# A transformer block on one core: the attention's row sums move from GpSimd to ScalarE

## The chip, the core and the metric

The kernel runs on one core of a Trainium2 chip. The metric is device time of one execution in microseconds (us). Five engines work side by side, each through its own instructions in order: TensorE (PE in the profile, PEld for its weight loads), VectorE (DVE), ScalarE (ACT), GpSimd (POOL) and SyncE (SP), which here issues every DMA. They wait for each other through semaphores. PSUM, where TensorE leaves its products, has eight banks of 128 x 512 f32.

## The reference

Input x is (8, 1024, 512) f32. Each token is layer-normed; the normed xn goes through causal attention with 16 heads of 32 and, in parallel, through a gated network whose inputs and weights are rounded to a 4-bit grid in blocks of 16. The result is the sum of three:

```python
xn = _layernorm(x, axis=-1)
x = x + _L0_attn_ref(xn, W_attn, b_attn, W_proj, b_proj) + _L0_ffn_ref(xn, w_gate, w_up, w_down)

# attention, per head
att = softmax(where(causal, q @ k.T * HD**-0.5, -inf));  y = att @ v
# fp4_quant_dequant, in blocks of 16 along the last dim
scale = max(max(abs(xb)) / 6, 1e-12)
q = GRID[searchsorted(MID, abs(xb / scale))] * sign(xb) * scale
# network
h = silu(fp4_linear(x, w_gate)) * fp4_linear(x, w_up);  return fp4_linear(h, w_down)
```

The softmax needs, for each row of scores, its maximum and the sum of its exponentials. The change is about that sum.

## The kernel before, in words

**Pieces.** The 8 batches x 1024 tokens are 64 tiles of 128 tokens; the 8 batches x 16 heads are 64 units of two heads (`HU = 2`). So a batch has eight tiles and eight units. Work on a tile: `prepare` (layer norm, transposes, `project` to q, k and v, which go to DRAM), `quantised` (the tokens rounded to the grid and transposed, `xqT`), `network` (three chunks of the hidden width 1408: `product` with the gate and up weights, `gated`, `hidden`, then `turn` and `down`) and `finish` (projection of the attention's y, sum with the network, output). Work on a unit: `maxima` and `weigh`.

**Maxima.** For 128 queries by up to 512 keys, `maxima` lets TensorE compute a block of scores in fp32r into a PSUM bank (L538, 24 blocks per unit), VectorE add the causal mask to the diagonal part (L546) and reduce to the negated row maximum (L548). The maxima of a unit are split into two fp32r parts, transposed (L564), stored to DRAM, and loaded as rows `shT`.

**Weights.** `weigh` computes the scores again, transposed: a matmul of `pick` and `shT` puts the negated maxima into the bank (L657), the matmul of `ks` and `qs` adds the scores (L660), ScalarE takes the exponential into `pr` in SBUF (L668), GpSimd clears what lies above the diagonal (L674), and TensorE multiplies by the values into y (L639). The inner `summed` lets GpSimd add the `pr` tiles into `sums` (L628, L633). At the end of each half Q of a unit, matmuls with `ones` sum over the partitions (L706); the sums go to DRAM, come back in `invert`, are inverted by VectorE and stored as `inverses`, which `finish` loads as `inv_y`.

**Quantising.** `Quantised` is a chain of VectorE operations on one 128 x 512 piece (L300 to L324). For the first `EARLY` = 28 of the 34 weight pieces, its two multiplications by a broadcast scale (L320, L324) run on GpSimd instead.

**What sets the order.** All instructions stand in an order written out by a planner in the program itself. It keeps a clock, dates at which each engine comes free (`act`, `dve`, `pool` add a planned cost), and the date at which each of six rotating PSUM banks comes back (`Banks`). Each piece of work is a generator that yields (TensorE's cost, the date from which it can go on, how many banks it needs); `merge` lets that stream go on that is least far in its own progress among those that can start. `Later` puts an action at a planned date. The chip has none of these dates: it runs each engine's instructions in the order that came out, and waits. Main stage: for unit n, `maxima` starts at progress n - 1.3, `weigh` at n, the network of tile n at n + 2, `finish` at n + 10, and the tiles two batches ahead are prepared in pairs. Before it lies a head in which the first 16 tiles are prepared and 28 weight pieces quantised.

In PSUM the six rotating banks serve all products but two, y and acc, which have a bank each.

Of the kernel before, what the change touches and what calls it, by code (L numbers as in the profile page):

```python
# [27 lines left out]
def kernel(  # L28
# [51 lines left out]
    QUEUE = 2.0  # L80
    SURE = 0.4
# [35 lines left out]
    ones = const.tile([P, HD], F32, name="ones")  # L117
    nc.gpsimd.memset(ones, 1.0)
# [66 lines left out]
    class Banks:  # L185


        def __init__(self):
            self.tiles = [ps_g.tile([P, W], F32, name=f"bank{k}") for k in range(6)]
            self.at = [0.0] * 6  # L190

# [3 lines left out]
        def take(self):  # L195
            k = self.at.index(min(self.at))
            assert self.at[k] < float("inf")
            self.at[k] = float("inf")
            return k, self.tiles[k]

        def back(self, k, time):
            self.at[k] = time

# [47 lines left out]
    class Quantised:  # L251
# [11 lines left out]
        def __init__(self, src, w, xs, after=0.0, helper=False):  # L263
# [6 lines left out]
            for wide, us, engine, action in self.operations(src, w, xs, helper):  # L270
                us = us + wide * w / CW
                self.left.append(Later(start, lambda us=us, engine=engine, action=action: self.one(us, engine, action)))
                start += SPREAD * us
# [8 lines left out]

        def done(self):
# [6 lines left out]
        def operations(self, src, w, xs, helper):  # L290
# [6 lines left out]
            spreader, name, cost = (nc.gpsimd, "pool", 1.35) if helper else (nc.vector, "dve", 0.7)  # L297
# [6 lines left out]
            def powers():  # L304
# [14 lines left out]
                (0.25, 0.72, "dve", scales),  # L319
                (cost, 0.0, name, lambda: spreader.tensor_tensor(blocks(xs), blocks(src), spread(inv), ALU.mult)),  # L320
                (1.14, 0.0, "dve", powers),
                (0.74, 0.0, "dve", lambda: nc.vector.tensor_tensor(xs, xs, step, ALU.add)),
                (0.78, 0.0, "dve", lambda: nc.vector.tensor_tensor(xs, xs, step, ALU.subtract)),
                (cost, 0.0, name, lambda: spreader.tensor_tensor(blocks(xs), blocks(xs), spread(scale), ALU.mult)),  # L324
# [12 lines left out]
    def weights_quantised():  # L337
# [15 lines left out]
        for k, piece in enumerate(pieces):  # L353
            raw = loaded.pop(0)
            done.append((piece, Quantised(raw, piece[4], raw, helper=k < EARLY)))
            while len(done) > (1 if k + 1 < len(pieces) else 0):
                (_, dst, r, c, w), wq = done.pop(0)
                yield 0.0, wq.ready(), 1
# [13 lines left out]
    def normed(tl):  # L372
# [9 lines left out]
        yield 0.0, pool(0.6, dve(1.4)), 0  # L382
        nc.vector.tensor_scalar(xt, xt, mv[:, 0:1], rstd, ALU.subtract, ALU.mult)
        tl.ready = dve(0.72)
# [25 lines left out]
    def quantised(tl):  # L410
# [6 lines left out]
        yield 0.0, xq.ready(), 1  # L417
# [5 lines left out]
    def project(batch, g, after):  # L423
        xnT = batch.xnT
        yield 0.0, after, 1
        for s in range(2):
            for f in range(0, NC, 2):
# [28 lines left out]
                def split(full=full, high=high, low=low):  # L456
                    nc.vector.tensor_copy(high, full)
                    nc.vector.tensor_tensor(low, full, high.bitcast(F32), ALU.subtract)
                    dve(1.3)
# [62 lines left out]
    def maxima(un):  # L522
# [3 lines left out]
        neg = p2.tile([P, 3, NK], F32, name="neg")  # L526
        for t in range(NT):
# [3 lines left out]
            for r in range(HU):  # L531
                k = i * HU + r
                for h in range(Q + 1):
                    n = W if h < Q else (i + 1) * P
                    bank, sc = banks.take()
# [12 lines left out]
                    nc.vector.tensor_reduce(neg[:, Q + h, k : k + 1], sc[:, :n], AX.X, ALU.max, negate=True)  # L548
                    end = dve(0.16 + 0.00103 * n, end)
                    banks.back(bank, end)  # L550
                    yield cost, free["dve"] - QUEUE, 1
        nc.vector.tensor_tensor(neg[:, 1, :], neg[:, 1, :], neg[:, 2, :], ALU.min)

        high = p2.tile([P, 2, NK], F32R, name="neg_high")
        stat = p2.tile([P, 2, 2, HU, QG], F32, name="stat")
        by_head = lambda a: a.rearrange("p (i r) -> p r i", r=HU)
        nc.vector.tensor_copy(high, neg[:, :2, :])
        for q in range(2):
            nc.vector.tensor_copy(stat[:, 0, q], by_head(high.bitcast(F32)[:, q, :]))
            nc.vector.tensor_tensor(stat[:, 1, q], by_head(neg[:, q, :]), stat[:, 0, q], ALU.subtract)  # L560
        rows = 2 * 2 * NK
        yield 0.0, dve(2.6), 1, 0.3
# [7 lines left out]
        def store():  # L570
            un.shift = dram.tile([2, 2, HU, W], F32, name="shift_kept")
            nc.sync.dma_start(out=un.shift.rearrange("e q r (i p) -> (e q r i) p", p=P), in_=statT)
            Later(2.5, load)
# [10 lines left out]
        yield 0.15, 0.0, 0, 0.3  # L584

    def weigh(un):
# [16 lines left out]

        def invert():
            flat = HU * S // P
            z = p2.tile([P, flat], F32, name="z")
            nc.sync.dma_start(out=z, in_=un.batch.sums[un.u].rearrange("q g (p e) -> (q g p) e", e=flat))
            inverses = un.batch.inverses[un.u].rearrange("q r (p e) -> (q r p) e", e=flat)
            Later(14.0, lambda: nc.vector.reciprocal(z, z))

            def store():
                nc.sync.dma_start(out=inverses, in_=z)
                un.batch.units_done += 1

            Later(16.0, store)

        for Q in range(2):
# [3 lines left out]
            sums = [p1.tile([P, W], F32, name=f"sum{r}") for r in range(HU)]  # L621

            def summed(group):

                for r in range(HU):
                    prs = [(pr, q0) for _, s, pr, q0 in group if s == r]
                    if group[0][0] == 0:
                        nc.gpsimd.tensor_tensor(sums[r], prs[0][0], prs[1][0], ALU.add)  # L628
                        pool(1.35)
                    else:  # L630
                        for pr, q0 in prs:
                            pool(0.2 + (W - q0) * 0.0022)
                            nc.gpsimd.tensor_tensor(sums[r][:, q0:], sums[r][:, q0:], pr[:, q0:], ALU.add)  # L633

# [16 lines left out]
            for j in range(last + 1):  # L651
# [45 lines left out]
                if j % 2 == 1:  # L697
                    summed(waiting)
            yield 0.0, max(ready, emptied, free["pool"] + HOP), 1
# [23 lines left out]
            def store(Q=Q, yu=yu, zs=zs):  # L723
# [8 lines left out]
                if Q == 1:  # L732
                    Later(8.0, invert)
# [385 lines left out]
```

## Time and profile before

| | us |
|---|---|
| median of 3 runs | 4801.91 (4801.69 to 4806.67) |
| the profiled execution | 4794.69 |
| its span | 4792.7 |
| TensorE busy | 4317.5 (90%) |
| VectorE busy | 3332.4 (70%) |
| GpSimd busy | 1942.2 (41%) |
| ScalarE busy | 1473.8 (31%) |
| granted TensorE clock, mean | 0.958 |

Busy time of an engine counts its instructions from start to end; matmuls overlap and their ends are modelled, so a TensorE that is shown busy is not at its peak. A row of the costliest groups reads: line, engine, operation, what is written and read, shape and count, then busy time and mean ns of one, then the idle time of the engine just before these instructions and what ended it. A row of the waits reads: who waited, for what, then us in total, times, and the longest. "PE bank L331 <- DVE xs L324" is TensorE idle before a transpose (L331) until VectorE's last operation (L324) on the tile `xs` had ended.

### The profile page before, as it was taken

Reading aid. Unit: us, or ns where it says so; the run is one execution under the profiler, and the core shown is the slowest. Engines: PE = TensorE matmul, PEld = TensorE weight load, DVE = VectorE, ACT = ScalarE, POOL = GpSimd, SP = SyncE. Lnnn points to the kernel's source line nnn. Section 1 sums busy time; section 2 is a strip of 40 time slices with the busy share of each in tenths; the row PEclk is TensorE's granted clock in tenths of the full one; section 3 lists DMA queues with packets and bytes.
Section 4 is the critical chain, followed back from the end, with each engine's and each line's share of the span. In section 5 each row is a group of like instructions: output and inputs, shape, how many; then the busy total and the mean of one; then the engine's idle time right before and its main releaser. Section 6 shows DMA issues by size and latency. Waiting matters only on the chain.

```text
span 4792.7 us, 59517 instructions
## 1 busy us (share of the span) xinstructions
PE 4317.5 (90%) x18708; PEld 2664.7 (56%) x18708; DVE 3332.4 (70%) x6883; ACT 1473.8 (31%) x2910; POOL 1942.2 (41%) x2632
## 2 busy tenths in 40 slices
PE   6566999999999999999999999999999899999994
PEld 5454555555565555556655555655555555555553
DVE  5556767777777777777777677777777777777752
ACT  1112333333333333333333333333333333333320
POOL 2213444444444444444444444443444444444430
PEclk8788999999999999999999999999999999999997
DMA  5655434435444544554454454545544333333213
GB/s 185 204 166 143 109 108 119 107 112 143 135 131 140 141 135 128 148 137 132 136 150 135 125 150 131 141 131 144 139 125 105 97 85 85 85 85 85 76 58 92
DMA packets 601659, 596.99 MB, mean 125 GB/s; under 512 B 133504, under 2 KB 457600, under 8 KB 601344
## 3 DMA queue, kind: packets, MB, share of 16 engines
q1 hardware_dynamic: 601344, 593.18, 44.9%
q8 instruction: 150, 2.46, 0.2%
q14 instruction: 165, 1.35, 0.1%
HBM read 423.11 MB, written 169.87 MB: 124 GB/s over the span
## 4 chain that ended last, share of the span: by engine, by line
PE 52%; DVE 25%; DMA 15%; SPq 3%; issue 3%; ACT 1%; POOL 0%; DVEq 0%; ACTq 0%; POOLq 0%
PE bank L785 16%; PE acc L763 6%; PE bank L878 4%; PE bank L538 4%; PE bank L657 4%; PE bank L433 4%; PE y L639 4%; PE bank L660 4%; DMA ks<-qk_kept 3%; DMA qk_kept<-full 3%; DMA inv_y<-inv_kept 3%; DMA qs<-qk_kept 3%; PE bank L331 2%; DVE step L308 2%; PE bank L477 2%
## 5 line engine op out<-in xcount | busy, mean ns | idle before, releaser
L633 POOL TENSOR_TENSOR sum<-sum,pr 128x512 f32<-128x512 f32 (+3 forms) x1024 | 1000.1, 987 | 428.8 <-ACT pr L668 392.9
L548 DVE TENSOR_REDUCE neg<-bank 128x1 f32<-128x512 f32 (+3 forms) x1536 | 840.9, 556 | 348.3 <-PE bank L538 312.3
L668 ACT ACTIVATE pr<-bank 128x512 f32<-128x512 f32 (+3 forms) x1536 | 674.9, 491 | 1022.6 <-PE bank L660 848.6
L674 POOL TENSOR_SCALAR_AFFINE_SELECT pr<-pr 128x128 f32<-128x128 f32 x1024 | 388.7, 393 | 1225.9 <-ACT pr L668 1217.8
L538 PE MATMUL bank<-ks,qs 128*128 128x512 f32 (+3 forms) x1536 | 703.9, 505 | 53.1 <-DMA ks<-qk_kept 17.7
L785 PE MATMUL bank<-wuT,xqT 128*128 128x512 f32 (+1 forms) x1536 | 682.3, 571 | 0.0
L763 PE MATMUL acc<-wdT,hqT 128*128 128x512 f32 x1408 | 677.3, 602 | 1.4 <-ACT hqT L332 1.4
L785 PE MATMUL bank<-wgT,xqT 128*128 128x512 f32 (+1 forms) x1536 | 660.5, 563 | 0.0
L657 PE MATMUL bank<-shT,pick 128*128 128x512 f32 (+3 forms) x1536 | 605.7, 402 | 31.0 <-ACT full L444 25.2
L546 DVE TENSOR_TENSOR bank<-bank,mask 128x128 f32<-128x128 f32 x1024 | 299.3, 292 | 447.5 <-PE bank L538 446.5
L628 POOL TENSOR_TENSOR sum<-pr 128x512 f32<-128x512 f32 x256 | 362.4, 1440 | 608.2 <-ACT pr L668 608.2
L660 PE MATMUL bank<-qs,ks 128*128 128x512 f32 (+3 forms) x1536 | 520.8, 348 | 0.0
L433 PE MATMUL bank<-xnT,wa 128*128 128x256 f32 x2048 | 480.2, 390 | 5.1 <-DMA wa<-in_L_attn_W_attn_dram 3.5
L538 PEld LDWEIGHTS bank<-ks,qs 128*128 128x128 f32 x1536 | 284.4, 191 | 328.3 <-issue 195.3
L433 PEld LDWEIGHTS bank<-xnT,wa 128*128 128x128 f32 x2048 | 397.4, 197 | 73.3 <-DMA wa<-in_L_attn_W_attn_dram 5.5
L657 PEld LDWEIGHTS bank<-shT,pick 128*128 128x128 f32 x1536 | 294.1, 191 | 221.1 <-issue 106.2
L785 PEld LDWEIGHTS bank<-wgT,xqT 128*128 128x128 f32 x1536 | 279.9, 191 | 233.7 <-issue 180.6
L785 PEld LDWEIGHTS bank<-wuT,xqT 128*128 128x128 f32 x1536 | 283.5, 195 | 205.6 <-issue 161.2
L763 PEld LDWEIGHTS acc<-wdT,hqT 128*128 128x128 f32 x1408 | 257.9, 191 | 225.0 <-issue 208.8
L639 PE MATMUL y<-pr,vs 128*32 128x512 f32 (+3 forms) x3072 | 361.7, 518 | 0.0
L660 PEld LDWEIGHTS bank<-qs,ks 128*128 128x128 f32 x1536 | 294.7, 192 | 60.8 <-issue 31.8
L444 ACT ACTIVATE full<-bank,bqk 128x256 f32<-128x256 f32 x256 | 107.5, 471 | 608.6 <-DMA qk_kept<-full 299.4
(88 smaller groups left out, 4899.7 us busy)
## 6 DMA issues: line engine op xcount, KB each, us to landing
wa<-in_L_attn_W_attn_dram SPq DMA_DIRECT2D x192, 512.0 KB
qs<-qk_kept SPq DMA_DIRECT2D x512, 128.0 KB
ks<-qk_kept SPq DMA_DIRECT2D x512, 128.0 KB
wp<-in_L_attn_W_proj_dram SPq DMA_DIRECT2D x81, 512.0 KB
qk_kept<-high SPq DMA_DIRECT2D x128, 256.0 KB
qk_kept<-full SPq DMA_DIRECT2D x128, 256.0 KB
y_kept<-yu SPq DMA_DIRECT2D x256, 128.0 KB
yT<-y_kept SPq DMA_DIRECT2D x128, 256.0 KB
```

The lines of the kernel that those rows point to most:

```text
L433: nc.tensor.matmul(pq[:, j, :], lhsT=wa[:, c, j * P : (j + 1) * P], rhs=xnT[:, c, :], start=(c == 0), stop=(c == NC - 1),)
L538: nc.tensor.matmul(sc[:, :n], lhsT=un.qs[Q][:, r, i * P : (i + 1) * P], rhs=un.ks[h][:, r, :n], start=True, stop=True,)
L548: nc.vector.tensor_reduce(neg[:, Q + h, k : k + 1], sc[:, :n], AX.X, ALU.max, negate=True)
L628: nc.gpsimd.tensor_tensor(sums[r], prs[0][0], prs[1][0], ALU.add)
L633: nc.gpsimd.tensor_tensor(sums[r][:, q0:], sums[r][:, q0:], pr[:, q0:], ALU.add)
L639: nc.tensor.matmul(y[row : row + HD, q0:], lhsT=un.vs[h][:, jj, r * HD : (r + 1) * HD], rhs=pr[:, q0:], start=(j < 2), stop=(j >= last - 1 ...
L657: nc.tensor.matmul(w[:, q0:], lhsT=pick[:, Q * HU + r, :], rhs=un.shT[:, q0:], start=True, stop=False)
L660: nc.tensor.matmul(w[:, q0:], lhsT=un.ks[h][:, r, jj * P : (jj + 1) * P], rhs=un.qs[Q][:, r, q0:], start=False, stop=True,)
L668: nc.scalar.activation(pr[:, q0:], w[:, q0:], AF.Exp)
L674: nc.gpsimd.affine_select(out=pr[:, q0 : q0 + P], in_=pr[:, q0 : q0 + P], compare_op=ALU.is_ge, fill=0.0, base=0, pattern=[[1, P]], channe ...
L763: nc.tensor.matmul(tl.acc, lhsT=job.hqT[:, j, :], rhs=wdT[:, i, :], start=(i == 0), stop=(i == NI - 1))
L785: nc.tensor.matmul(job.g, lhsT=job.tl.xqT[:, c, :], rhs=wT[:, c, job.i0 : job.i0 + job.w], start=(c == 0), stop=(c == NC - 1),)
```

## The change

1. In `maxima`, after each block's maximum, ScalarE takes the exponential of the block in place in its PSUM bank, with the block's own negated maximum as bias, and gives the row sums through `accum_out`. The bank comes back after that. At a unit's end the two partial sums of a row are brought to the common maximum (`least`, `gap`, one small exponential), added, inverted, and transposed and stored together with the maxima (48 rows instead of 32).
2. `summed` on GpSimd, the ones matmuls, the copies `zs`, and the way of the sums through DRAM go. `yu` gets two buffers.
3. All weight pieces are quantised by VectorE alone.
4. In the planner: banks that are held are tracked; a stream that waits for a quantised tile asks again until the planned end has passed (`wait`); several planned costs of VectorE are lower; `units_done` counts when y is stored.

```diff
+    LATE = 0.6
...
-    ones = const.tile([P, HD], F32, name="ones")
-    nc.gpsimd.memset(ones, 1.0)
...
         def take(self):
-            k = self.at.index(min(self.at))
-            assert self.at[k] < float("inf")
+            while len(self.held) == len(self.tiles):
+                passed(0.2)
+            k = min((k for k in range(len(self.tiles)) if k not in self.held), key=self.at.__getitem__)
             self.at[k] = float("inf")
+            self.held.add(k)
             return k, self.tiles[k]
+        def expect(self, k, time):
+            self.at[k] = time
...
+        def wait(self):
+            while self.ready() > clock[0] + 0.05:
+                yield 0.0, self.ready(), 1
...
-            spreader, name, cost = (nc.gpsimd, "pool", 1.35) if helper else (nc.vector, "dve", 0.7)
...
-            done.append((piece, Quantised(raw, piece[4], raw, helper=k < EARLY)))
+            done.append((piece, Quantised(raw, piece[4], raw)))
...
-                yield 0.0, wq.ready(), 1
+                yield from wq.wait()
...
         xq = Quantised(xs, D, xs)
-        yield 0.0, xq.ready(), 1
+        yield from xq.wait()
...
+        sums = p2.tile([P, 3, NK], F32, name="row_sums")
+        older = []
+        def summed(bank, sc, n, kind, k):
+            nc.scalar.activation(
+                sc[:, :n],
+                sc[:, :n],
+                AF.Exp,
+                bias=neg[:, kind, k : k + 1],
+                accum_out=sums[:, kind, k : k + 1],
+            )
+            banks.back(bank, act(n, 0.0, "exp") + 0.27)
+            free["act"] += 0.27
...
-                    banks.back(bank, end)
+                    block = (bank, sc, n, kind, k)
+                    older.append(Later(end - clock[0] + LATE, lambda block=block: summed(*block)))
+                    banks.expect(bank, end + LATE + 0.9)
+                    while len(older) > 3:
+                        older.pop(0).now()
                     yield cost, free["dve"] - QUEUE, 1
-        nc.vector.tensor_tensor(neg[:, 1, :], neg[:, 1, :], neg[:, 2, :], ALU.min)
+        yield 0.0, end + LATE + 1.0, 0
+        settle(older)
+        least = p2.tile([P, NK], F32, name="least")
+        nc.vector.tensor_tensor(least, neg[:, 1, :], neg[:, 2, :], ALU.min)
+        gap = p2.tile([P, 2, NK], F32, name="gap")
+        for part in range(2):
+            nc.vector.tensor_tensor(gap[:, part, :], least, neg[:, 1 + part, :], ALU.subtract)
+        yield 0.0, dve(0.6), 0
+        nc.scalar.activation(gap, gap, AF.Exp)
+        yield 0.0, act(2 * NK, 0.0, "exp"), 0
+        nc.vector.tensor_tensor(sums[:, 1:, :], sums[:, 1:, :], gap, ALU.mult)
+        nc.vector.tensor_tensor(sums[:, 1, :], sums[:, 1, :], sums[:, 2, :], ALU.add)
...
+            nc.vector.reciprocal(stat[:, 2, q], by_head(sums[:, q, :]))
...
+            nc.sync.dma_start(
+                out=un.batch.inverses[un.u].rearrange("q r (i p) -> (q r i) p", p=P), in_=statT[2 * 2 * NK :, :]
+            )
...
-            sums = [p1.tile([P, W], F32, name=f"sum{r}") for r in range(HU)]
-            def summed(group):
-                for r in range(HU):
-                    prs = [(pr, q0) for _, s, pr, q0 in group if s == r]
-                    if group[0][0] == 0:
-                        nc.gpsimd.tensor_tensor(sums[r], prs[0][0], prs[1][0], ALU.add)
-                        pool(1.35)
-                    else:
-                        for pr, q0 in prs:
-                            pool(0.2 + (W - q0) * 0.0022)
-                            nc.gpsimd.tensor_tensor(sums[r][:, q0:], sums[r][:, q0:], pr[:, q0:], ALU.add)
...
-            yield 0.0, max(ready, emptied, free["pool"] + HOP), 1
+            yield 0.0, max(ready, emptied), 0
...
-                    nc.tensor.matmul(
-                        z[row : row + HD, :],
-                        lhsT=ones,
-                        rhs=sums[r][:, half * W // 2 : (half + 1) * W // 2],
...
-            nc.scalar.copy(zs, z)
...
-                    nc.sync.dma_start(out=un.batch.sums[un.u, Q, g : g + 1, :], in_=zs[g * HD : g * HD + 1, :])
-                if Q == 1:
-                    Later(8.0, invert)
+                un.batch.units_done += Q
```

## The prediction

> **What bounds the kernel now.** I read the page's engine totals first, then busy time by stretch, then TensorE's own waits, and last the rows of the groups that the change touches.
>
> ```profile
> PE 4317.5 (90%) x18708; PEld 2664.7 (56%) x18708; DVE 3332.4 (70%) x6883; ACT 1473.8 (31%) x2910; POOL 1942.2 (41%) x2632
> ```
>
> ```profile
> 0.00:370.00 370.00, 230.17 (x972) 187.80 (x973) 196.96 (x417) 60.92 (x126) 76.14 (x89) 0.82 0.60 185
> 370.00:720.00 350.00, 300.16 (x1355) 188.53 (x1353) 241.10 (x522) 113.26 (x233) 150.08 (x215) 0.92 0.43 118
> 720.00:4600.00 3880.00, 3661.41 (x15995) 2211.53 (x15995) 2828.78 (x5818) 1287.74 (x2530) 1702.37 (x2312) 0.98 0.45 122
> 4600.00:4793.00 193.00, 125.75 (x391) 76.83 (x389) 65.58 (x128) 11.87 (x23) 13.61 (x17) 0.85 0.26 78
> ```
>
> The columns of the stretches are PE, PEld, DVE, ACT, POOL busy, granted clock, DMA share, GB/s. From 720 to 4600 us, 81% of the run, TensorE is busy 3661 of 3880 us (94%). ScalarE is busy 33% there and GpSimd 44%, so neither bounds by its sum. What TensorE waits for in that stretch is therefore what can be won:
>
> ```profile
> PE bank L331 <- DVE xs L324: 186.5, 59, 9.2
> ...
> PE bank L331 <- POOL hid L324: 75.8, 14, 12.1
> ```
>
> The first row is the run's: 59 times TensorE stands some 3 us before the transposes of a tile's quantised tokens, because VectorE has not finished them. From 720 on it is 169.6 of the 219 us that TensorE is idle. The second lies wholly before 370 us: transposes of the weights wait for GpSimd's share of the quantising.
>
> Why VectorE is late shows in two stretches of its timeline, the same three operations beside a busy GpSimd and alone:
>
> ```profile
> 2531.47 1.69 POOL L757 TENSOR_TENSOR res<-res,bp 128x512 f32<-128x512 f32 x1
> 2533.13 4.01 POOL L633 TENSOR_TENSOR sum<-sum,pr 128x512 f32<-128x512 f32 x3
> ...
> 2531.96 1.42 DVE L305 TENSOR_SCALAR step<-hid 128x384 int32<-128x384 int32 x1
> 2533.42 1.31 DVE L308 TENSOR_SCALAR step<-step 128x384 f32<-128x384 f32 x1
> 2534.76 1.24 DVE L322 TENSOR_TENSOR hid<-hid,step 128x384 f32<-128x384 f32 x1
> ...
> 4655.82 0.36 DVE L305 TENSOR_SCALAR step<-hid 128x384 int32<-128x384 int32 x1
> 4656.22 0.36 DVE L308 TENSOR_SCALAR step<-step 128x384 f32<-128x384 f32 x1
> 4656.61 0.56 DVE L322 TENSOR_TENSOR hid<-hid,step 128x384 f32<-128x384 f32 x1
> ```
>
> 0.36 us becomes 1.42 until a GpSimd instruction ends. Reductions out of PSUM keep their time (687 ns at 512 columns throughout).
>
> **The change, part by part.** The profiled execution took 4794.7 us (span 4792.7), 7.2 us (0.15%) under the median of 4801.9; the sum is made against 4794.7 and the forecast moved up by about that.
>
> *The ones matmuls go.*
>
> ```profile
> L706 PE MATMUL bank<-sum,ones 128*32 128x256 f32 x1024 | 105.9, 385 | 0.7 <-POOL sum L633 0.6
> ...
> 2502.97 0.63 PE L639 MATMUL y<-pr,vs 128*32 128x256 f32 x8
> 2503.22 0.80 PE L706 MATMUL bank<-sum,ones 128*32 128x256 f32 x8
> 2503.96 1.98 PE L763 MATMUL acc<-wdT,hqT 128*128 128x512 f32 x4
> ```
>
> 128 groups of eight passes. The row says 0.83 us each, but ends are modelled: from the start of the y group to the start of L763 two groups of the same width take 0.99 us, so one is 0.5 us. 128 x 0.5 = 64; ends 55 (0.43, a full pass of the same columns elsewhere) and 106. I take **-62**. With them go 128 copies of 379 ns on ScalarE, the round trip of the sums through DRAM (576 issues net on SP) and the planned wait for GpSimd before the last y group; all idle-covered, 0.
>
> *VectorE is freed.* GpSimd loses L633 (1000.1), L628 (362.4) and 62.9 us of weight quantising: 1942 - 1425 = 517 us stay (mask of the probabilities, bias, rstd). Count x (mean - time alone) over the quantising rows (L300, L302, L305, L308, L320 to L324) and L383 is about 350 us of delay; in proportion to GpSimd's busy time 27% stays, so 257 us go. VectorE gains 56 weight multiplications at 0.69 or 0.55 (38 us) and per unit net six operations on 8 to 16 columns at about 0.24 (92 us): 3332 - 257 + 130 = 3205 us, still about 69%.
>
> *The wait for the tokens.* Its place is decided by the instruction order too, because the changed kernel asks again until the planned end has passed. I laid the two orders side by side, with 0.43 us for a 512-column f32 pass and 0.23 for fp32r on TensorE and VectorE's times alone: from the maxima's matmul that VectorE must see first to the tile's transposes, TensorE has 8.9 and 11.1 us of work in alternate tiles of the kernel before, against 10.3 and 10.8 on VectorE: short by 1.4 every second tile before any delay by GpSimd. In the changed order it is 16.3 and 12.8 against 13.8 and 13.2: 2.5 spare, then short by 0.4. Ends: all 186 goes, or only the delay by GpSimd (six long operations of a tile, 4.5 us by their means against 3.6 alone: 64 x 0.9 = 58). I take **-150**, nearer the first, since both causes shrink; what is late next is banks, below.
>
> *The weights' quantising in the head.* Up to 75.8 us of waits for GpSimd go, 38 us of VectorE's work come, and the head is also paced by the store of `full` (120.8 us of ScalarE's waits before 370 us). Ends -76 and +38; I take **-20**.
>
> *ScalarE's new exponentials.* 1536, in the shapes of L668 (491 ns mean). L444 at 256 columns with a bias by partition takes 471, L668 at 256 without takes 386: +85. Reading out the sum is in no row: 0 to 244 ns (L566, the smallest operation). So 0.58 to 0.82 us each, 885 to 1260 us; I count 0.82, the dear end, for capacity. ScalarE then has 1474 - 49 + 1260 + 18 (one small exponential per unit) = 2703 us, 58%: covered in sum. The built program has 188 table loads in both orders, so no further 1283 ns switch is paid.
>
> *Banks.* Each block now keeps its bank through VectorE and ScalarE. At 512 columns that is 0.69 + 0.68 + up to 0.24, where it was 0.69. In the order before, one of some 4,400 bank reuses comes sooner (in TensorE's work) than the earlier reader needs with empty queues; in the changed order 144 do, together 73 us short, mostly runs of maxima in the head and after the last preparations. Below: 0, if other delays cover them; above: twice 73, if queues double it. I take **+65**.
>
> The nearest page rule speaks against this part. The Trainium skill, ScalarE: Activation LUTs, § Step-by-step, holds that ScalarE writes faster to PSUM than to SBUF but that this is useful only if TensorE does not need most of PSUM. Here TensorE uses six banks in rotation plus y and acc, so by the rule I would put the longer hold at its upper end, 146, and the sum at -61 (4734); by the rows it stays at 65 and the sum at -142. No row here shows an in-place exponential.
>
> *ScalarE's order.* Each new exponential waits for a VectorE maximum; behind it stand the exponentials of the weights, and behind those the y matmuls and banks. TensorE's work between the last scores of a group and its y matmuls falls from a median of 7.8 us to 5.4, at the lowest tenth from 3.8 to 2.1; one pair needs about 0.6 + 0.6 + 0.4 (L674). Tight for a tenth of 384 groups. Below 0 (ScalarE now waits 774 us for the scores, so it has room); above 150 (0.1 us per new exponential). I take **+25**.
>
> *The longer end of a unit's maxima* (gap, exponential, rescale: about 3 us) is covered: maxima are planned to begin 1.3 units, some 90 us, ahead of their use. VectorE's multiplication by the gap waits for that exponential, and quantising is queued behind it; in every second unit the order puts nothing between, so VectorE stands for ScalarE's queue, an estimated 1 to 2 us 32 times. VectorE is idle 30%; I count 0 and leave the 64 to the range. The tail from 4691 us is a serial chain of loads and projections, untouched: 0.
>
> Sum: -62 - 150 - 20 + 65 + 25 = **-142**: 4794.7 - 142 = 4652.7, about **4657** on the median's scale.
>
> **The rivals.**
> A, *more goes than counted*: all TensorE waits on quantising go and banks are hidden: -62 - 186 - 60 + 20 = -288, 4510. For it: the waits named are nearly all of the idle time. Against: 144 short reuses.
> B, *the waits move*: tokens are ready but ScalarE's queue makes TensorE wait as long: -62 - 60 - 10 + 110 = -22, 4780.
> C, *slower*: ScalarE blocks in order. A late maximum holds the weights' exponentials, which hold y and the banks. It decides when TensorE loses more than 232 us (62 + 150 + 20) to it, 0.15 us per new exponential; at 0.2 us it is 307 - 232 = +75, 4875. For it: 58% of ScalarE in strict order, y slack cut by a third. Against: VectorE's dates become truer as its delays go, and ScalarE stands idle 42%.
> D, *the delay stays*: the 517 us left on GpSimd still hit the quantising; only half of the token wait goes: 4794.7 - 62 - 90 + 70 = 4713.
>
> **How the numbers follow.** Forecast (with D inside its range, 4590 to 4740) 0.60; A 0.17; B 0.10, of which 0.03 within 0.2% (10 us, about what this kernel's runs can tell); C 0.13. Faster 0.83, same 0.03, slower 0.14. The range leaves out the far half of A below and most of C above: 4525 to 4800. The likeliest case alone: 4590 to 4740.
>
> **What would show it.** Right: "PE bank L331 <- DVE xs" under 60 us; L308 at 512 columns near 430 ns on average instead of 598; POOL near 500 us; new exponentials between 0.58 and 0.82 us; TensorE's busy time down by some 100 us. Wrong: "PE ... <- ACT" rows of over 200 us, or ScalarE waiting for `neg` while scores stand ready (C); token waits that stay over 120 us (D); a head longer than 370 us.

## The result, and the profile after

| | before | after |
|---|---|---|
| median, us | 4804.29 | 4856.87 (4850.69 to 4859.2) |
| ratio to before | 1 | 1.0104, 95% interval 1.0086 to 1.0121 |
| profiled execution / span, us | 4794.69 / 4792.7 | 4856.44 / 4854.4 |

The changed kernel is 1.0% slower; the forecast was 4657 us in a range of 4525 to 4800. The profile does not look like a loss at first. These are the engine totals, two groups of the new operation and one of the quantising rows, from the page and the groups of the changed kernel:

```profile
PE 4380.8 (90%) x17684; PEld 2641.3 (54%) x17684; DVE 3021.9 (62%) x7323; ACT 2317.5 (48%) x5918; POOL 510.3 (11%) x1295
L542 ACT ACTIVATE bank<-bank,neg 128x512 f32<-128x512 f32 (+3 forms) x1536 | 860.2, 563 | 266.1 <-DVE neg L574 261.1
L542 ACT ACTIVATION_READ_ACCUMULATOR bank<-bank,neg 128x1 f32 x1536 | 322.4, 210 | 0.0
L319 DVE TENSOR_SCALAR step<-step 128x512 f32<-128x512 f32 (+1 forms) x290 | 119.8, 413 | 10.0
```

GpSimd is down to 510 us and VectorE's delay beside it is gone (the operation of the last row took 625 ns on average before). A new exponential is recorded with 563 ns and its read-out with 210, but the records lie partly over each other: in a run without the 1536 of them (e11, below) ScalarE is busy 886 us less than with them (e1), which is 0.58 us each. No engine has a larger share of the span than before except ScalarE, which stands idle half the time. TensorE is shown busy 63 us longer, where the forecast had some 100 us less. The main stage of the changed kernel (columns PE, PEld, DVE, ACT, POOL busy, granted clock, DMA share, GB/s) shows it no better fed:

```profile
720.00:4600.00 3880.00, 3645.09 (x14798) 2149.87 (x14799) 2485.93 (x6070) 2007.75 (x5138) 439.71 (x1124) 0.97 0.45 121
```

Why, TensorE's waits in the changed kernel say (total us, times, longest):

```profile
PE bank L782 <- ACT full L455: 77.0, 17, 4.7
...
PE bank L677 <- ACT bank L542: 39.9, 38, 2.6
PE bank L564 <- DMA ks<-qk_kept: 39.2, 24, 2.4
PE bank L564 <- DMA qs<-qk_kept: 36.9, 27, 5.3
...
PE bank L564 <- ACT bank L542: 20.1, 72, 1.3
```

The token wait (186.5 us before) is down to 0.2 us. In its place stand a gate product (L782) that waits for ScalarE's copy into the tile `full` in `project` (L455), scores (L564) that wait for the loads of queries and keys, and scores and weights (L564, L677) that wait for the new exponentials. All rows "PE ... <- ACT full" make 136 us, all "PE ... <- ACT bank L542" 71.

One of the 17 stands, in the timeline of the changed kernel (start, us, what):

```profile
2795.80 0.84 ACT L455 ACTIVATE full<-bank,bqk 128x256 f32<-128x256 f32 x2 [2.71 <-PE bank L444]
...
2800.51 1.07 PE L659 MATMUL y<-pr,vs 128*32 128x512 f32 x8
...
2800.75 0.41 SPq L474 DMA_DIRECT2D qk_kept<-full  x1
...
2805.27 0.84 ACT L455 ACTIVATE full<-bank,bqk 128x256 f32<-128x256 f32 x2 [8.06 <-DMA qk_kept<-full]
...
2806.16 9.19 PE L782 MATMUL bank<-wgT,xqT 128*128 128x384 f32 x16 [4.58 <-ACT full L455]
```

`project` has one buffer `full`. ScalarE's next copy into it stands 8.06 us for the store of the last one to land; ScalarE goes in order, so its new exponentials stand behind it too. The bank that this copy is to empty is the one that the order gives to the gate product, and TensorE stands 4.58 us. That ScalarE stands for the store is not new. Its waits before and after, and between them TensorE's largest wait for the copy before:

```profile
ACT full L444 <- DMA qk_kept<-full: 299.4, 44, 10.1
...
PE bank L657 <- ACT full L444: 25.2, 19, 3.9
```

```profile
ACT full L455 <- DMA qk_kept<-full: 317.0, 49, 11.0
```

What the stand costs is more than itself. The granted clock in the same stretch (columns PE busy, clock, DMA share, GB/s):

```profile
2800.00:2802.00 2.00, 1.58 (x13) 1.00 0.48 124
2802.00:2804.00 2.00, 0.00 (x0) 1.00 0.98 326
2804.00:2806.00 2.00, 0.00 (x0) 0.81 0.55 205
2806.00:2808.00 2.00, 1.84 (x3) 0.50 0.26 87
2808.00:2810.00 2.00, 2.00 (x4) 0.50 0.88 299
2810.00:2812.00 2.00, 2.00 (x4) 0.50 0.03 8
2812.00:2814.00 2.00, 2.00 (x6) 0.99 0.00 0
```

For six microseconds after it TensorE runs at half clock (the weight loads of its products come 0.64 us apart, and 0.43 once the clock is back): some three more are lost. The Trainium skill, TensorE: Matmul & The Clock Gate, § Part 1: The HAM clock gate, says that the clock is halved after an idle window of some 3.4 us and comes back after a busy one; this row agrees with the fall, and with a return within two such windows.

### The profile page after: what moved, and what is told of

Read it like the earlier page. It is cut to its first block, busy times and chain, and to the rows that moved or that the text cites. A ratio compares the mean times of both kernels' runs of the same rounds, so it can differ in the third digit from the quotient of the medians.

```text
span 4854.4 us, 58995 instructions
## 1 busy us (share of the span) xinstructions
PE 4380.8 (90%) x17684; PEld 2641.3 (54%) x17684; DVE 3021.9 (62%) x7323; ACT 2317.5 (48%) x5918; POOL 510.3 (11%) x1295
## 4 chain that ended last, share of the span: by engine, by line
PE 72%; DMA 12%; DVE 6%; SPq 5%; ACT 3%; issue 2%; ACTq 0%; POOL 0%; DVEq 0%; POOLq 0%
PE bank L782 21%; PE acc L760 10%; PE bank L444 8%; PE y L659 6%; PE bank L677 6%; PE bank L564 5%; PE bank L680 5%; PE bank L875 5%; DMA qk_kept<-full 4%; PE bank L488 3%; SPq L516 3%; PE bank L342 2%; DMA qs<-qk_kept 2%; DMA ks<-qk_kept 2%; DMA xs<-xn_kept 2%
## 5 line engine op out<-in xcount | busy, mean ns | idle before, releaser
L542 ACT ACTIVATE bank<-bank,neg 128x512 f32<-128x512 f32 (+3 forms) x1536 | 860.2, 563 | 266.1 <-DVE neg L574 261.1
L564 PE MATMUL bank<-ks,qs 128*128 128x512 f32 (+3 forms) x1536 | 699.9, 495 | 114.1 <-DMA ks<-qk_kept 39.2
L782 PE MATMUL bank<-wgT,xqT 128*128 128x512 f32 (+1 forms) x1536 | 700.7, 592 | 77.3 <-ACT full L455 77.0
L694 POOL TENSOR_SCALAR_AFFINE_SELECT pr<-pr 128x128 f32<-128x128 f32 x1024 | 368.6, 371 | 3338.0 <-ACT pr L688 3327.7
L677 PE MATMUL bank<-shT,pick 128*128 128x512 f32 (+3 forms) x1536 | 641.1, 425 | 65.5 <-ACT bank L542 39.9
L782 PE MATMUL bank<-wuT,xqT 128*128 128x512 f32 (+1 forms) x1536 | 683.5, 573 | 9.6 <-ACT bank L542 9.5
L564 PEld LDWEIGHTS bank<-ks,qs 128*128 128x128 f32 x1536 | 286.2, 194 | 437.3 <-issue 216.0
L444 PE MATMUL bank<-xnT,wa 128*128 128x256 f32 x2048 | 502.8, 403 | 18.9 <-DMA wa<-in_L_attn_W_attn_dram 10.5
L782 PEld LDWEIGHTS bank<-wgT,xqT 128*128 128x128 f32 x1536 | 298.4, 204 | 325.9 <-issue 189.9
L444 PEld LDWEIGHTS bank<-xnT,wa 128*128 128x128 f32 x2048 | 411.4, 204 | 95.9 <-issue 19.5
L677 PEld LDWEIGHTS bank<-shT,pick 128*128 128x128 f32 x1536 | 291.7, 190 | 279.0 <-issue 91.2
L455 ACT ACTIVATE full<-bank,bqk 128x256 f32<-128x256 f32 x256 | 107.5, 471 | 698.0 <-DMA qk_kept<-full 317.0
L782 PEld LDWEIGHTS bank<-wuT,xqT 128*128 128x128 f32 x1536 | 282.3, 194 | 244.3 <-issue 180.7
L542 ACT ACTIVATION_READ_ACCUMULATOR bank<-bank,neg 128x1 f32 x1536 | 322.4, 210 | 0.0
```

The lines of the kernel that those rows point to most:

```text
L444: nc.tensor.matmul(pq[:, j, :], lhsT=wa[:, c, j * P : (j + 1) * P], rhs=xnT[:, c, :], start=(c == 0), stop=(c == NC - 1),)
L542: nc.scalar.activation(sc[:, :n], sc[:, :n], AF.Exp, bias=neg[:, kind, k : k + 1], accum_out=sums[:, kind, k : k + 1],)
L564: nc.tensor.matmul(sc[:, :n], lhsT=un.qs[Q][:, r, i * P : (i + 1) * P], rhs=un.ks[h][:, r, :n], start=True, stop=True,)
L677: nc.tensor.matmul(w[:, q0:], lhsT=pick[:, Q * HU + r, :], rhs=un.shT[:, q0:], start=True, stop=False)
L694: nc.gpsimd.affine_select(out=pr[:, q0 : q0 + P], in_=pr[:, q0 : q0 + P], compare_op=ALU.is_ge, fill=0.0, base=0, pattern=[[1, P]], channe ...
L782: nc.tensor.matmul(job.g, lhsT=job.tl.xqT[:, c, :], rhs=wT[:, c, job.i0 : job.i0 + job.w], start=(c == 0), stop=(c == NC - 1),)
```

## The experiments

All times are medians of four runs beside seven of the kernel before on the same chip; line numbers differ by a few between kernels. Differences below are of medians; by the ratios they are up to 16 us smaller or larger, which is said where it matters.

| run | kernel | us | ratio (95%) |
|---|---|---|---|
| e1 | after, two buffers `full`, `high` | 4685.27 | 0.9775 (0.9758 to 0.9793) |
| e2 | before, two buffers | 4757.79 | 0.9925 (0.9903 to 0.9947) |
| e3 | after, exponentials over one column | 4827.95 | 1.0069 (1.0051 to 1.0086) |
| e4 | before, the planner asks again | 4607.17 | 0.9610 (0.9593 to 0.9626) |
| e5 | e4, two buffers | 4548.80 | 0.9482 (0.9456 to 0.9507) |
| e6 | e5, weights quantised by VectorE | 4574.60 | 0.9525 (0.9490 to 0.9559) |
| e7 | e1, exponentials over one column | 4658.94 | 0.9707 (0.9682 to 0.9732) |
| e8 | after without the exponentials | 4609.12 | 0.9604 (0.9578 to 0.9629) |
| e9 | after, not asking again | 5123.39 | 1.0663 (1.0638 to 1.0688) |
| e10 | e1, planned costs of before | 4676.25 | 0.9723 (0.9693 to 0.9753) |
| e11 | e1 without the exponentials | 4572.69 | 0.9523 (0.9496 to 0.9550) |
| e12 | e5 without ones matmuls, new order | 4690.17 | 0.9767 (0.9747 to 0.9787) |
| e13 | e5 without ones matmuls, same order | 4485.92 | 0.9360 (0.9346 to 0.9374) |
| e14 | e12, landing date for the loads | 4520.22 | 0.9426 (0.9405 to 0.9447) |
| e15 | e1, landing date | 4623.76 | 0.9640 (0.9624 to 0.9656) |
| e16 | e11, landing date | 4417.72 | 0.9212 (0.9191 to 0.9233) |
| e17 | e5, landing date | 4487.80 | 0.9360 (0.9341 to 0.9379) |
| e18 | e7, landing date | 4596.94 | 0.9584 (0.9561 to 0.9608) |

### The store of `full` (e1, e2, e3)

Theory: ScalarE's copy, standing for the store, is what the order hands on to TensorE. Rival: ScalarE's new work itself is too much. e1 and e2 give the two tiles a second buffer; the instruction orders stay those of after and of before.

```diff
-                full = p1.tile([P, 2, QW], F32, name="full")
+                full = p2.tile([P, 2, QW], F32, name="full")
...
-                high = p1.tile([P, 2, QW], F32R, name="high")
+                high = p2.tile([P, 2, QW], F32R, name="high")
```

> The changed kernel with two buffers instead of one for the tiles full and high of project; every engine's instruction order is as in the changed kernel. Store theory (ScalarE stands in its order for the DMA that empties the single full buffer, TensorE's next product needs the bank that this ScalarE copy reads, and after 4 to 5 us of standing the granted clock is 0.5 for some 5 us): the waits of TensorE for full (about 113 us with all rows) go, and some 50 us of halved clock with them: 4857 - 150 = about 4705 us, between 4680 and 4740. Load theory (ScalarE's longer work and the longer held banks cost the time by themselves, the buffer is incidental): within 30 us of 4857.

> The same two buffers in the kernel before (zs has one buffer instead of two, for room); instruction order as in the kernel before. Store theory in the form that the change made this wait matter: TensorE waits only some 25 us for full here, so 10 to 40 us go: 4765 to 4795. Rival, the buffer was worth as much before the change: 150 us go, 4655.

e3 leaves the tiles and shortens each new exponential.

```diff
             nc.scalar.activation(
-                sc[:, :n],
-                sc[:, :n],
+                sc[:, :1],
+                sc[:, :1],
```

> The changed kernel with each new exponential over one column of its block instead of all (it leaves out nearly all of the row sums); orders, waits and bank use unchanged. It takes some 0.28 us from each of 1536 operations, 430 us of ScalarE's time. Store theory: the stands for the store stay, 4825 to 4857. Load theory: 80 us or more go, under 4780.

e1 takes 172 us off the changed kernel (158 by the ratios): the rows for `full` fall from 136 to 4 us of TensorE's waits, and the kernel is then faster than before. The same edit is worth 38 us in the kernel before. In e3 ScalarE loses 464 us of work, and the wait stays what it was, in TensorE's waits of e3:

```profile
PE bank L782 <- ACT full L455: 77.4, 17, 4.7
```

It gains 29 us (17 by the ratios). So of these two the store, not ScalarE's time for the exponentials, is by far the larger. What the longer holds of banks cost, e3 does not say: it leaves them as they are.

### Asking again (e4, e5, e9)

Does the token wait need GpSimd's lighter load, or only the planner's new question? e4 puts the question alone into the kernel before, at its three places:

```diff
+        def wait(self):
+            while self.ready() > clock[0] + 0.05:
+                yield 0.0, self.ready(), 1
...
-        yield 0.0, xq.ready(), 1
+        yield from xq.wait()
```

> The kernel before with one part of the change alone: a stream that waits for a quantised piece asks again until its planned end has passed. Prediction's step on the token wait, order part: TensorE's 186 us of waits for the tokens fall below 90 and the time by about 100, 4690 to 4740. Rival, the wait only moves to another place: 4780 to 4810.

e5 adds the two buffers. e9 takes the question out of the changed kernel.

> The kernel before with asking again (as in e4_before_wait) and two buffers for full and high. Row sums stay on GpSimd. Store theory: of e4's TensorE waits, 36 us are for full; they go with little clock loss: 4607 - 40 = about 4567, between 4545 and 4590. Rival: the two gains are the same gain, and it stays within 12 us of 4607.

> The changed kernel without asking again: a stream goes on at the date first planned for its quantised piece, as in the kernel before. Alone in the kernel before, asking again was worth 189 us. If the parts add, 4857 + 189 = about 5045, 4980 to 5080, with waits for the tokens of over 100 us. If the lower load of GpSimd had already freed VectorE, so that the tokens are ready without it (the prediction's other cause), under 4900.

e4 gains 189 us, more than expected, while GpSimd stays busy 1957 us and VectorE's operation beside it stays slower than in the changed kernel (548 ns by this group of e4, 413 there and 625 before; below it, TensorE's waits in e4):

```profile
L313 DVE TENSOR_SCALAR step<-step 128x512 f32<-128x512 f32 (+1 forms) x290 | 158.8, 548 | 10.0
```

```profile
PE bank L543 <- ACT full L449: 28.5, 18, 3.0
...
PE bank L336 <- DVE xs L329: 3.0, 2, 1.6
```

The tokens' row is down from 186.5 to 3.0 us by the order alone. The rows for `full`, 41 us before, are 55 in all, among the largest that are left; e5 takes these too. Without the question the changed kernel loses 267 us, more than the parts added up, and tokens come back as its first row:

```profile
PE bank L342 <- DVE xs L335: 172.5, 36, 12.9
PE bank L342 <- DVE hid L335: 79.4, 13, 15.8
PE bank L782 <- ACT full L455: 78.4, 17, 4.7
```

So GpSimd's lighter load alone did not free the tokens; that rival falls.

### The weights (e6)

```diff
-            done.append((piece, Quantised(raw, piece[4], raw, helper=k < EARLY)))
+            done.append((piece, Quantised(raw, piece[4], raw, helper=False)))
```

> As e5_wait_full2, and all weights quantised by VectorE alone, the change's third part. Prediction's step on the head (-20, ends -76 and +38): e4 still shows 33 us of TensorE's waits for GpSimd's quantising in the head; 0 to 33 us less than e5. Rival: VectorE's 38 us of added work lengthen the head: up to 38 us more.

26 us slower than e5. TensorE's waits in the head, e5 and then e6:

```profile
PE bank L336 <- POOL hid L329: 26.4, 11, 7.3
...
PE bank L336 <- DVE xt L388: 17.5, 10, 8.1
...
PE bank L336 <- DVE hid L329: 10.1, 4, 5.3
```

```profile
PE bank L336 <- DVE xt L388: 49.2, 11, 9.3
PE bank L336 <- DVE hid L329: 23.7, 10, 5.3
```

The wait for GpSimd becomes one for VectorE, which normalises the first tiles (`xt`) at the same time, and grows. The wait to be won was small by then: of the 75.8 us for GpSimd in the kernel before, e4 and e5 have 33 and 26.

### The exponentials (e7, e8, e10, e11)

e7 is e3 with two buffers. e8 (one buffer) and e11 (two) give the bank back after the maximum and set the sums to one, so the row sums are left out:

```diff
+        nc.gpsimd.memset(sums, 1.0)
...
-                    older.append(Later(end - clock[0] + LATE, lambda block=block: summed(*block)))
-                    banks.expect(bank, end + LATE + 0.9)
+                    banks.back(bank, end)
```

e10 is e1 with the planner's VectorE costs of before.

> The changed kernel with two buffers and each new exponential over one column (nearly all of the row sums left out); orders as in the changed kernel. What ScalarE's time for the exponentials still costs once the store no longer holds it: load theory, 60 us or more under 4685. Theory that the longer plan-time hold of banks (fixed by the order written out) is what remains: within 30 us of 4685.

> The changed kernel without the new exponentials: a block's bank comes back after its maximum, the row sums are left out (set to one). One buffer for full as in the changed kernel. It has all that the change removes and nothing of what it adds on ScalarE per block. If banks held longer made TensorE meet the store, its waits for full fall under 40 us and the time to e4 less the ones matmuls (about 60): 4530 to 4590. If the lighter GpSimd and the planner's lower costs themselves cost time, above 4640.

> The changed kernel with two buffers for full and high, and the planner's costs of VectorE as in the kernel before (scales 0.25/0.72, powers 1.14, 0.74, 0.78, 1.4, 0.72, 1.3, 1.9). Only dates in the plan differ from e1. Theory that the lower costs bring the maxima's matmuls ahead of the loads of q and k (TensorE's waits for them are 87 us in e1, 36 in the kernel before): the waits fall under 50 and the time by 30 to 60, 4625 to 4655. Rival, the banks held longer set it: within 20 us of 4685 or slower.

> The changed kernel without the new exponentials (row sums set to one, banks back after the maximum) and with two buffers for full and high. Against e1 (4685) it sizes the exponentials with their longer holds when the store is out of the way. Theory: banks held longer cost 60 to 110 us there (e7 showed ScalarE's time to be 26): 4575 to 4625. Rival, the store was all: within 30 us of 4659, the time of e7.

The exponentials cost 113 us in e1 against e11, of which their length is 26 (e7). e8 came 19 us above its range, though the waits for `full` had fallen to 35 us in all. Those are still worth 36 us (e11), and another wait had grown, which stays in e11:

```profile
PE bank L564 <- DMA qs<-qk_kept: 84.2, 35, 7.7
...
PE bank L564 <- DMA ks<-qk_kept: 55.2, 31, 2.9
```

139 us for the loads of queries and keys; in e5 it is 38, in e1 87. The lower planned costs have little part in the time: e10 is 9 us faster than e1 by the medians (25 by the ratios), and its waits for these loads are 75 us.

### The loads, and what the ones matmuls were worth (e12 to e14)

e13 and e12 take the ones matmuls out of e5 (the sums are set to one): e13 lets the planner think that they are there, e12 does not.

```diff
-                    nc.tensor.matmul(
-                        z[row : row + HD, :],
-                        lhsT=ones,
...
-            yield cost + 0.45, 0.0, 2
+            yield cost, 0.0, 2
```

(The last edit, with the bank and the earlier request for it, in e12 alone.)

> The kernel before with the planner asking again and two buffers for full and high (4548.8 us), now without the 128 groups of ones matmuls, of their bank and of the 0.45 us that the planner gives them; GpSimd's additions stay, but their result is not used: the row sums are set to one, which is left out of the computation. It asks what the prediction's first term (-62) was worth once the waits for tokens and the store are out of the way. If that term holds: 64 to 55 us less, 4485 to 4495. If the time of the ones matmuls is taken up again by waits for the loads of queries and keys, as the runs without the new exponentials suggest (139 us of such waits against 38): 4520 to 4550, with those two rows together above 80 us.

> As e12 (no ones matmuls, row sums set to one, which is left out of the computation), but the planner still gives them their bank and their 0.45 us, so that every engine's order is that of e5 (4548.8 us). If the loss in e12 came from the planner's new order: the prediction's first term shows, 64 to 55 us less than e5, 4485 to 4500, with waits for qs and ks near e5's 38 us. If TensorE without these matmuls simply runs into the loads: 4540 or more, with those waits above 80 us.

In the same order the 128 groups are worth 63 us, as predicted. In the new order taking the work away costs 141, which neither expectation of e12 had. TensorE's waits of e12, then of e13:

```profile
PE bank L543 <- DMA qs<-qk_kept: 132.8, 39, 14.4
```

```profile
PE bank L543 <- DMA ks<-qk_kept: 24.7, 20, 1.8
...
PE bank L543 <- DMA qs<-qk_kept: 19.4, 4, 11.9
```

`maxima` asks only whether its loads were put on SP, not whether they have landed. In e12 its stream runs a little further ahead, right up to that line. The timeline of e12 (one stand of many):

```profile
1826.88 1.73 SPq L510 DMA_DIRECT2D qs<-qk_kept  x4
...
1831.31 0.76 PE L543 MATMUL bank<-ks,qs 128*128 128x512 f32 x1 [3.29 <-DMA qs<-qk_kept]
```

e14 gives the planner a date for it, and nothing else:

```diff
             lst.append(tl)
+        un.landed.append(clock[0] + 6.0)
...
+            while un.landed[Q] > clock[0] + 0.05:
+                yield 0.0, un.landed[Q], 1
```

> As e12 (order laid anew, no ones matmuls, row sums set to one), but the planner holds the second half of a unit's maxima until 6 us after its loads of queries and keys were put on SP. If the waits for these loads are what made e12 slow (165 us of waits for qs and ks, and the clock that falls to 0.50 after each stand of 3 us): those two rows together under 60 us and 4490 to 4560. If the new order loses elsewhere: above 4620.

170 us come back; the rows for `qs` and `ks` are down to 12 us. The loss in e12 was the order against the loads, but for the 34 us by which e14 stays above e13.

### The same date in the changed kernel, and the price of the exponentials without it (e15 to e18)

> The changed kernel with two buffers for full and high (e1, 4685.3 us), and the planner holds the second half of a unit's maxima until 6 us after its loads were put on SP. If the loads cost the changed kernel what their waits show (87 us, and the lower clock after the longer ones): the rows of qs and ks under 40 us together, 4600 to 4650. If they only cover waits for banks, which then come in their place: 4670 to 4700.

> The changed kernel with two buffers and the landing date (e15, 4623.8 us), without the new exponentials, the banks given back after the maximum, row sums set to one (the sums are left out of the computation). If the exponentials and longer holds cost what the prediction summed, 65 + 25: 90 less, 4520 to 4550. If their price in e1 against e11 was right: 113 less, 4500 to 4520; since e11 waited 139 us for loads against e1's 87, the price can also be larger: 4460 to 4500.

> The kernel before with the planner asking again, two buffers for full and high (e5, 4548.8 us) and the landing date for the loads. e5 waited 38 us for those loads: at best 4510, or 4530 to 4560 if the order laid anew costs what the waits gave. If row sums on ScalarE were worth having with everything else repaired, it would be above e15's 4623.8.

> The changed kernel with two buffers and the landing date (e15, 4623.8 us), each new exponential over one column instead of up to 512, so that its row sums are left out of the computation; the planner's order is e15's. ScalarE loses some 460 us and the banks come back some 0.3 us sooner. If the price of the exponentials (206 us, e15 against e16) is ScalarE's time in its order: half of it or more goes, 4440 to 4520. If it lies in the order laid for longer holds: 4580 to 4624; e7 against e1 gave 26 us, which would be 4598.

e15 gains 62 us on e1. Against it e16 shows the exponentials and longer holds at 206 us, more than any theory had: in e1 and e11 the waits for the loads had hidden half of it. Of the 206, e18 gives back 27. The stretch 720 to 4300 us of e15, then of e16 (columns as above):

```profile
720.00:4300.00 3580.00, 3490.60 (x14293) 2086.64 (x14292) 2381.27 (x5857) 1933.86 (x4959) 411.76 (x1076) 0.97 0.47 127
```

```profile
720.00:4300.00 3580.00, 3535.67 (x14948) 2138.48 (x14947) 2513.10 (x6114) 1236.32 (x2432) 445.47 (x1187) 1.00 0.47 130
```

TensorE gets through 655 fewer matmuls in the same time, idle only 45 us more. The clock takes a larger part: 0.974 against 0.998 before rounding, some 85 us of 3580. Over the whole execution the mean clock is 0.958 in e15 and 0.976 in e16, some 90 us. Where, e15's timeline shows in a run of maxima, one block at a time as ScalarE gives the banks back, after two table loads of 1.28 us (the second is shown; e15 and e16 both have 188 of them):

```profile
2003.73 1.28 ACT L543 ACT_TABLE_LOAD   x1
...
2005.02 0.66 ACT L543 ACTIVATE bank<-bank,neg 128x512 f32<-128x512 f32 x1
...
2005.61 0.19 ACT L543 ACTIVATION_READ_ACCUMULATOR bank<-bank,neg 128x1 f32 x1
2005.70 0.65 ACT L543 ACTIVATE bank<-bank,neg 128x512 f32<-128x512 f32 x1
...
2005.86 0.50 PE L567 MATMUL bank<-ks,qs 128*128 128x512 f32 x1 [0.90 <-ACT bank L543]
...
2006.52 0.38 PE L567 MATMUL bank<-ks,qs 128*128 128x256 f32 x1 [0.17 <-ACT bank L543]
...
2007.19 0.74 PE L567 MATMUL bank<-ks,qs 128*128 128x512 f32 x2 [0.29 <-ACT bank L543]
```

and the clock there (columns PE busy, clock, DMA share, GB/s):

```profile
2004.00:2006.00 2.00, 1.10 (x5) 1.00 0.20 75
2006.00:2008.00 2.00, 1.48 (x4) 1.00 0.33 131
2008.00:2010.00 2.00, 1.79 (x4) 0.60 0.00 0
2010.00:2012.00 2.00, 2.00 (x5) 0.50 0.00 0
```

The waits are all under 1.3 us, yet the clock falls as after a long stand. This is no single case. From 720 us on, the trace's record of the clock has 39 falls in e15, 24 of them with no stand of TensorE of 1 us or more in the 6.8 us before; these 24 alone take 77 us of clock. With short exponentials (e18) there are 22 such falls, which take 51 us; in e16 and in e17 there is one each.

e17 repairs the kernel before in the same three ways: 4487.8 us, less than expected, 6.4% (6.2 to 6.6%) under the kernel before and 136 us under e15. With these three repairs on both sides, the rest of the change, row sums on ScalarE above all, still loses.

## Why the prediction was wrong

The sum was -62 - 150 - 20 + 65 + 25. By its steps:

- **The ones matmuls, -62: right**, where the order is kept (e13, -63). The prediction took it as time that simply falls out of TensorE. In a program whose planner lays the order anew that holds only if nothing else is late; e12 lost 141 instead.
- **The wait for the tokens, -150: right in what goes, wrong in what it takes.** The row fell from 186.5 to 0.2 us; asking again alone is worth 189 us (e4). The half of the argument that leaned on GpSimd's lighter load was not needed.
- **VectorE is freed: right** (3022 us, below the 3205 worked out; 429 ns for the operation of L319 at 512 columns, where near 430 was forecast), **and worth nothing** that any run shows by itself.
- **The weights, -20: wrong sign**, +26 (e6) where asking again had already taken more than half of the wait for GpSimd. The upper end of the range, +38, was the nearer row: VectorE in the head was already awaited for `xt`.
- **The exponential's price, 0.58 to 0.82 us: the cheap end was right.** It is 0.58 us of ScalarE's time; the prediction counted the dear end, 2703 us of ScalarE in all, and 2317 came. The rule of the Trainium skill that was weighed for the banks (ScalarE: Activation LUTs, § Step-by-step) pointed the right way, and the sum made by it, 4734 against 4653 by the rows, lay nearer. The rule says nothing on the store, and the holds cost more than the upper end taken for it, 146.
- **ScalarE's order, +25: right in size** by what shortening the exponentials brings back (26 to 29 us in e3, e7 and e18; 17 to 33 by the ratios), but not by the route: the y matmuls, which were to wait behind late exponentials, wait 1.1 us for `pr` in the changed kernel.
- **Banks, +65: mis-sized.** Holds and order together cost 206 us (e16 to e15), 179 of them still there with short exponentials. The count of reuses that come too soon (144, 73 us) saw each as its own delay. It put them into runs, mostly in the head and after the last preparations; in e15 30 of the 41 us for which score matmuls (L567) wait for a bank from ScalarE lie between 720 and 3500 us. And it did not see that a run of short waits halves the clock.
- **The step that is missing decides the sign: the store of `full`.** The prediction wrote "what is late next is banks", and named the store only for the head; past it the store has no term in the sum. That ScalarE waited 299 us for it stood in the trace of before; TensorE hardly felt it then (25.2 us in the largest row, 41 in all). In the changed kernel the same copy waits 317 us, and the order hands TensorE that very bank: 136 us of waits, and 172 us in the time (e1). With the loads (62 us, e15) the two waits cost the changed kernel 233 us; in e4 the same two repairs are worth 119 (e17).

Put together, on the way from before over e4, e17 and e15 to after: asking again -197 (from 4804), two buffers and landing dates -119, the rest of the change +136, and the two repairs taken out again +233: +53. The +136 are 70 won by what is removed (e17 to e16, the weights' loss inside it) and 206 lost to exponentials and holds. Another order of the steps would split the sum otherwise, as e12 and e13 show.

Rival C came near in time (4875) and its sign, "PE ... <- ACT" rows above 200 us, came true (136 + 71). Its mechanism did so only in part: it let a late maximum hold up ScalarE, and with it y and the banks. ScalarE did wait 261 us for maxima, and TensorE waited 71 us for banks from its new exponentials; but the larger part, 136 us, came from a DMA, y waited 1.1 us, and shorter exponentials gained 29 us. That the time came near is luck in so far.

**Open.** Of the 179 us that stay with short exponentials, some 50 are clock lost after runs of short waits; no run tells the order laid for longer holds from the passage of every bank through ScalarE's queue. Why the planner's order ran closer to the loads in the changed kernel than in e5 (87 against 38 us) is not settled either; the lower planned costs explain at most 12 of the 87 (75 in e10).

## What to carry to other kernels

Before a wait is removed, follow the engines that wait but are not yet awaited: an engine that stands in order for a store (ScalarE for `full`, 299 us) can cost little (38 us here) until the new order makes another engine wait for what it holds, and a second buffer is then worth four times what it was. Where a program plans its own order, a term is measured in the order kept and in the order laid anew (63 us won and 141 lost by the same removal), and every transfer gets a landing date. Price a stand of TensorE of 3 us or more, or a run of short ones, with the lower clock after it.

## What the runs showed of the hardware

- A stand of 4.6 us was followed by six microseconds at a granted clock of 0.50; after the stand of 3.29 us for loads in e12, the clock was 0.50 from 1832 to 1836 us.
- The clock also fell to 0.50 without any stand above 1.3 us: in e15 TensorE was busy 1.10 and 1.48 us of two stretches of 2 us, and then ran at half clock, and 24 falls from 720 us on have no stand of 1 us before them. The rule cited above names an idle window; here TensorE was busy for more than half of the 4 us before.
- Reading out the row sum is an instruction of its own on ScalarE, recorded with 210 ns each and 322 us in all, but most of it lies over its neighbours: in the rows of e15 above, two exponentials of 512 columns with a read-out between them start 0.68 us apart.
- Whether the activation gained from writing to PSUM is not shown: it took 672 ns at 512 columns with the bias, against 602 for the exponential into SBUF without one. With a bias both, at 256 columns, it took 456 ns against 471 for L455, which is another function.
